# The nine taps of a 3x3 convolution, dealt out over two steps or four of a scan pipeline

## The chip, the core and the metric

The kernel runs on one core of one Trainium2 chip. The metric is the device time of one execution in microseconds (us). The chip's engines are named as in the profile: PE is TensorE's matmul and PEld its weight load, DVE is VectorE, ACT is ScalarE, POOL is GpSimd, SP is SyncE, which issues DMAs. "L468" is line 468 of the kernel before.

## What is computed

The program runs four layers, each of the form `x = x + layer(group_norm(x))`, on x of shape (8, 128, 64, 64) in float32. The change is in layer 0. Layer 0 splits the 128 channels in two halves. The first 64 go through a selective state-space scan along the 4096 pixels of an image; the last 64, `x_hw`, go through a plain 3x3 convolution. Cut to what matters:

```python
x_id, x_hw = (x[:, :GC], x[:, GC:])                  # GC = 64
t = x_id.transpose(0, 2, 3, 1) @ expand_w @ concat_w + concat_b
xs, z = split(_ln(t) @ in_w + in_b)                  # 128 channels each
xc = silu(causal_conv1d(xs))                         # 3 taps along the pixels
dt, Bm, Cm = projections(xc)                         # Bm, Cm: N = 16 states
dA  = exp(dt[..., None] * A)
dBx = dt[..., None] * Bm[:, :, None, :] * xc[..., None]
h_t = dA_t * h_{t-1} + dBx_t;  y_t = sum_n h_t[:, n] * C_t[n]
y = (y + xc * D_ssm) * silu(z)
x_id_out = (t + y @ out_w + out_b).transpose(0, 3, 1, 2)
hw = conv3x3(x_hw, conv_w) + conv_b                  # 'SAME' padding
return relu(concatenate([x_id_out, hw], axis=1))
```

Layer 1 then runs four sweeps of a 1x9 convolution over rows and columns, one row after another; layers 2 and 3 are convolutions and a deformable convolution with gathered samples.

## The kernel before

Layer 0 is worked off in 32 **chunks** of 1024 pixels (16 image rows): four chunks per image, eight images. A chunk has two halves of 512 pixels (T = 512), one PSUM bank each in float32. The scan needs 128 channels times 16 states = 2048 lanes, that is 16 groups of 128 partitions per half, and a **step** of the pipeline handles two groups. So a half takes 8 steps and a chunk 16, and the whole scan 512 steps, one after another in a single loop (L629). Chunk c owns steps 16c to 16c+15; below, "step 14" is the fifteenth of its chunk's own steps, at `t0 + 14` with `t0 = 16 * c`.

In step i, the loop issues in this order:

- `step_scan(i)` (L578): DVE multiplies the products u of the two groups with B, in PSUM (L583), and runs two scans (L594) into a tile `hb` (four buffers).
- `layer1.add(i)`: in the second half of the layer, DVE's part of a layer-1 row.
- `step_u(i + 1)` and `step_dt(i + 2)` (both through `spread`, L559): PE spreads 8 channels over 128 lanes, for u and for dt, by two products each. I call the four together the **spread products**. u has two double banks at first; from step `shared` = 280 on it has one, and the other is lent to layer 1. dt has one double bank.
- `step_carry(i - 1)` (L600, ACT): the last column of `hb`, for the next half.
- `step_decay(i + 2)` (L576): ACT takes the exponential of dt.
- `step_weigh(i - 1)` (L605): POOL multiplies `hb` with C.
- the **events** of step i (L643): everything else that has to be done for some chunk, put down beforehand in a table by `at(step, function)`.
- in odd steps, `round_sum(i - 3)` (L613): PE adds up the states of steps i-3 and i-2, four products; I call it the **group sum**. It waits for POOL's weighing, and it frees two `hb` buffers, for which the scans of steps i+1 and i+2 wait.
- `layer1.products(i)` (L724): once layer 1 has begun (step 294 on, images 0 to 3), nine products of one of its rows.

Each engine works its own queue in this order. The events of a chunk begin 33 steps before its scan (load, normalization, the products of the input side) and end 24 steps after its first scan step. So several chunks' events fall into each step. In terms of the chunk whose scan runs, PE's events by step are: ps_x in steps 0 and 1 (three products each, L386), ps_bc and ps_z in steps 2 and 3, ps_o in step 4, ps_v in 5 and 6, ps_t in 7, ps_var in 8, ps_bc again in 10 and 11, and the 3x3 convolution, ps_c, in steps 14 and 15. All these products share one PSUM bank (pool `pg`, L155, one buffer): the next may begin when an engine has read the one before. Where the chunk before was the last of its image (chunks 4, 8, 12, ...), the events of step 12 contain `out_norm` (L507), put down with the chunk before and so ahead of the chunk's own: DVE makes the mean and variance of the finished image, with two tiny products (ps_gn L272, ps_gv L280) between DVE's instructions.

The convolution (`conv_taps`, L458) takes the taps one by one, the middle one first: a tap is two products (one for each half of the chunk) of the 64 input channels in the upper 64 partitions of `xn` with a 64x64 weight, added up in ps_c. After the last tap ACT reads the two halves of ps_c into `res` (L476). Its planning is:

```python
at(t0 + 14, also(conv_taps, taps[0:5]))
at(t0 + 15, also(conv_taps, taps[5:9]))
```

## Time and profile before

| what | us |
|---|---|
| three timed runs: lowest, median, highest | 7635.89, 7638.51, 7647.05 |
| the profiled execution | 8068.85 |
| its span, first to last instruction | 8066.5 |
| layer 0's scan, from the first L583 to the last, in the profiled execution | 95.5 to 3157.4 |
| of it before layer 1 shares TensorE | to about 1600 |
| busy in the span: PE, DVE, POOL, ACT | 6262.5, 4469.1, 4114.6, 3505.2 |

The profiled execution is longer than the timed runs, so shares and durations come from it and the comparison of kernels from the timed runs. A row of the profile's groups names the line, the engine, the operation, the tiles (result first, then operands), the shape and the count, then the busy time and the mean duration, and last the engine's idle time ahead of these instructions and what ended it. A product in float32 shows as two records. "PEclk" is the clock that TensorE was granted, as a share of full speed; at 0.5 a product takes twice as long.

| groups of layer 0 | count | mean ns |
|---|---|---|
| L583 DVE, product with B | 512 | 1221 |
| L594 DVE, scan | 896 and 128 | 1267 and 1208 |
| L605 POOL, weighing with C | 512 | 2379 |
| L576 ACT, exponential | 512 | 1024 |
| L468 PE, convolution taps (two shapes) | 1152 in all | 646 and 634, overlapping |
| L476 ACT, reading ps_c | 64 | 682 |

### The profile page before, as it was taken

The page shows a single profiled execution, that of the slowest core. Times are in us where ns is not written, and L with a number is a line of the kernel's source. Part 1 is how long each engine was busy: PE and PEld are TensorE (multiplying, and loading weights), DVE is VectorE, ACT ScalarE, POOL GpSimd, SP SyncE. Part 2 cuts the span into 40 slices and gives each one's busy share as a digit, 9 for nine tenths or more (in the row PEclk, how much of TensorE's full clock was granted, in tenths as well). Part 3 has the DMA queues.
Part 4 walks back from the last instruction along what each step waited for, and adds up shares of the span by engine and source line. Part 5 has one row for each costly group of instructions (what it writes and reads, how often), then busy time and mean ns, then how long its engine had stood idle before and what let it go on. Part 6 is the DMA issues. An engine that isn't in the chain of part 4 may idle for free. (4 is left out here: it accounts for less than half of the span.)

```text
span 8066.5 us, 87137 instructions
## 1 busy us (share of the span) xinstructions
PE 6262.5 (78%) x30226; PEld 4059.5 (50%) x30226; DVE 4469.1 (55%) x5384; ACT 3505.2 (43%) x8218; POOL 4114.6 (51%) x3325
## 2 busy tenths in 40 slices
PE   6777878799999999538999999974467777676661
PEld 1222222255555556416777777753355555555551
DVE  4887887666666655111556545555445454454445
ACT  4554555433333331021444444444355555555453
POOL 3766666544444443111445444445565666666664
PEclk9887888799999999869999999987689888888785
DMA  1010110100000000131455455455566666666557
GB/s 41 26 44 26 38 36 28 35 12 24 21 19 18 17 14 9 54 118 51 150 174 160 155 163 158 152 163 172 170 201 194 207 195 201 192 199 201 177 176 259
DMA packets 333015, 897.77 MB, mean 111 GB/s; under 512 B 55464, under 2 KB 90544, under 8 KB 330528
## 3 DMA queue, kind: packets, MB, share of 16 engines
q0 software_dynamic: 184320, 604.13, 24.7%
q1 hardware_dynamic: 143648, 271.31, 10.3%
q10 hardware_dynamic: 4608, 16.78, 0.5%
q8 instruction: 239, 3.92, 0.2%
q14 instruction: 200, 1.64, 0.1%
HBM read 770.80 MB, written 121.21 MB: 111 GB/s over the span
## 5 line engine op out<-in xcount | busy, mean ns | idle before, releaser
L605 POOL TENSOR_TENSOR hb<-hb,bc 128x1024 f32<-128x1024 f32 x512 | 1216.4, 2379 | 1360.9 <-ACT carry L600 979.1
L1105 POOL DMA_INDIRECT X<-table,idx x1332 | 1272.1, 955 | 799.8 <-PE ps_s L1137 350.1
L1105 POOL DMA_INDIRECT got<-table,idx x972 | 930.0, 957 | 1083.8 <-ACT samp L1140 439.8
L594 DVE TENSOR_TENSOR_SCAN hb<-da,carry,u_ps 128x512 f32<-128x512 f32 x896 | 1098.0, 1267 | 275.8 <-PE ps_y L613 224.7
L576 ACT ACTIVATE da<-dt_ps 128x1024 f32<-128x1024 f32 x512 | 524.3, 1024 | 1316.0 <-PE dt_ps L559 1315.6
L1148 PE MATMUL ps_o<-samp,dcn_w 128*128 128x256 f32 x2304 | 676.4, 436 | 418.7 <-ACT samp L1140 224.0
L1137 PE MATMUL ps_s<-ident,X 128*128 128x128 f32 x5328 | 794.9, 308 | 241.2 <-DVE X L1123 144.7
L1140 ACT COPY samp<-ps_s 128x384 f32<-128x384 f32 x768 | 365.1, 475 | 1412.6 <-PE ps_s L1137 1033.7
L1123 DVE TENSOR_TENSOR X<-prod,X 128x768 f32<-128x768 f32 x444 | 425.2, 958 | 966.1 <-ACT X L1116 805.6
L1137 PEld LDWEIGHTS ps_s<-ident,X 128*128 128x128 f32 x5328 | 767.3, 221 | 303.1 <-DVE X L1123 161.7
L1116 ACT ACTIVATE X<-X,wgt 128x128 f32<-128x128 f32 x2664 | 826.1, 392 | 0.0
L559 PE MATMUL u_ps<-u,m_u 32*128 32x512 f32 x2048 | 639.3, 703 | 194.4 <-DVE hb L594 193.4
L1148 PEld LDWEIGHTS ps_o<-samp,dcn_w 128*128 128x128 f32 x2304 | 470.2, 214 | 554.2 <-ACT samp L1140 251.2
L583 DVE TENSOR_TENSOR u_ps<-u_ps,bc 128x1024 f32<-128x1024 f32 x512 | 625.2, 1221 | 182.1 <-PE dt_ps L559 165.3
L1116 ACT ACTIVATE got<-got,wgt 128x128 f32<-128x128 f32 x1944 | 611.2, 392 | 193.6 <-DMA got<-table,idx 189.9
L559 PE MATMUL dt_ps<-dt,m_dt 32*128 32x512 f32 x2048 | 642.5, 706 | 17.6 <-ACT da L576 17.6
L1121 DVE TENSOR_TENSOR prod<-X,prod 128x768 f32<-128x768 f32 x444 | 426.5, 961 | 117.4 <-ACT prod L1095 69.3
L1125 DVE TENSOR_TENSOR prod<-prod,got 128x384 f32<-128x384 f32 x324 | 183.6, 567 | 506.3 <-ACT got L1116 453.7
L559 PEld LDWEIGHTS u_ps<-u,m_u 32*128 32x128 f32 x2048 | 166.3, 198 | 553.2 <-DVE hb L594 365.9
L1121 DVE TENSOR_TENSOR prod<-got,prod 128x768 f32<-128x768 f32 x324 | 309.6, 955 | 145.7 <-DMA got<-table,idx 96.0
L1137 PE MATMUL ps_s<-ident,got 128*128 128x128 f32 x1944 | 296.1, 293 | 109.5 <-issue 47.6
L876 PE MATMUL ps_t<-xn,w 128*128 128x512 f32 (+4 forms) x688 | 317.3, 611 | 81.1 <-DVE t L907 56.6
(224 smaller groups left out, 10218.1 us busy)
## 6 DMA issues: line engine op xcount, KB each, us to landing
x<-x1d SPq DMA_DIRECT2D x128, 256.0 KB
table<-tok SPq DMA_DIRECT2D x128, 256.0 KB
X<-table,idx POOLq DMA_INDIRECT x1332
x<-x2d SPq DMA_DIRECT2D x48, 384.0 KB
x3h<-x3d SPq DMA_DIRECT2D x16, 1056.0 KB
x_st<-in_x SPq DMA_DIRECT2D x64, 256.0 KB
x_o<-in_x SPq DMA_DIRECT2D x64, 256.0 KB
x1d<-res SPq DMA_DIRECT2D x64, 256.0 KB
```

Source lines behind the costliest of these rows:

```text
L559: nc.tensor.matmul(ps[:, j, :], lhsT=mask[q, r].rearrange("p d n -> p (d n)"), rhs=S[c][src, h][q, :], start=True, stop=True,)
L576: nc.scalar.activation(da, steps[i]["dt"], AF.Exp)
L583: nc.vector.tensor_mul(st["bc"], st["bc"], s["bc", h][:, 0].unsqueeze(1).to_broadcast([P, 2, T]))
L594: nc.vector.tensor_tensor_scan(hb[:, j, :], st["da"][:, j, :], st["bc"][:, j, :], start, ALU.mult, ALU.add)
L605: nc.gpsimd.tensor_mul(hb, hb, S[c]["bc", h][:, 1].unsqueeze(1).to_broadcast([P, 2, T]))
L1105: nc.gpsimd.indirect_dma_start(out=got[:, k, :, :].rearrange("p q c -> p (q c)"), out_offset=None, in_=tab, in_offset=bass.IndirectOffsetO ...
L1116: nc.scalar.activation(got[:, k, q, :], got[:, k, q, :], AF.Identity, scale=wgt[:, t, k0 + k, q : q + 1])
L1121: nc.vector.tensor_mul(prod, got[:, :, 0:2, :], w.unsqueeze(3).to_broadcast([P, G3, 2, C]))
L1123: nc.vector.tensor_add(got[:, :, 0:2, :], prod, got[:, :, 2:4, :])
L1137: nc.tensor.matmul(ps[:, k, :], lhsT=got[:, k, q, :], rhs=self.ident, start=(q == 0), stop=(q == halves - 1))
L1140: nc.scalar.copy(samp[:, :, col : col + P], ps)
L1148: nc.tensor.matmul(ps, lhsT=self.dcn_w[:, k, :], rhs=samp[:, k - k0, :], start=(k == 0), stop=(k == KK - 1))
```

## The change

The nine taps are called in four parts of 3, 2, 2 and 2 taps, in steps 12, 13, 14 and 15, in place of two parts of 5 and 4 taps in steps 14 and 15. The order of the taps, the products themselves, the bank they add up in and the two ACT instructions after the last tap are the same. The bank and the tile `res` are asked for at the first part, so two steps earlier.

```diff
-                at(t0 + 14, also(conv_taps, taps[0:5]))
-                at(t0 + 15, also(conv_taps, taps[5:9]))
+                for i, ks in enumerate((taps[0:3], taps[3:5], taps[5:7], taps[7:9])):
+                    at(t0 + 12 + i, also(conv_taps, ks))
                 at(t0 + 20, y_product)
```

## The prediction

> **What bounds the kernel now.** I read the page's slices first, then engine shares by stretch, TensorE's waits, and TensorE's order of time around the convolution.

> ```profile
> PE   6777878799999999538999999974467777676661
> ...
> PEclk9887888799999999869999999987689888888785
> ```

> One digit is a fortieth of the span, 202 us. Layer 0 is the first 16 digits, in two regimes: to about 1535 us PE is 60 to 80% busy at a reduced clock, then 90% or more.

> ```profile
> core 0: us, PE busy (x) PEld busy (x) DVE busy (x) ACT busy (x) POOL busy (x), PEclk, DMA share, GB/s
> 640.00:1360.00 720.00, 575.23 (x2456) 151.62 (x2454) 589.63 (x525) 386.05 (x587) 485.09 (x254) 0.85 0.10 33
> 1658.00:3156.00 1498.00, 1464.29 (x7192) 878.49 (x7189) 923.76 (x944) 507.60 (x788) 682.79 (x357) 0.99 0.05 18
> ```

> In the first regime DVE is busy 82% and PE 80%: neither is full, so they take turns being late. In the second, where layer 1 shares TensorE (its first step is scan step 280 + 14 = 294), PE is busy 98%.

> ```profile
> PE u_ps L559 <- DVE hb L594: 170.9, 99, 4.9
> ...
> PE u_ps L559 <- DVE hb L594: 0.8, 2, 0.4
> ```

> These are TensorE's waits for the scan, first of 175 to 1535 us, then of 1658 to 3156 us (total us, times, longest). PE has holes in the first regime only. Where they lie is seen in chunk 11, steps 13 to 16:

> ```profile
> 1021.10 0.70 PE L559 MATMUL u_ps<-u,m_u 32*128 32x512 f32 x2 [1.65 <-DVE hb L594]
> ...
> 1026.14 1.05 PE L613 MATMUL ps_y<-hb,m_y 128*32 128x512 f32 x4 [2.93 <-POOL hb L605]
> ...
> 1028.20 4.47 PE L468 MATMUL ps_c<-xn,conv 64*64 64x512 f32 x20
> ...
> 1033.67 3.60 PE L468 MATMUL ps_c<-xn,conv 64*64 64x504 f32 x16
> 1037.20 1.06 PE L613 MATMUL ps_y<-hb,m_y 128*32 128x512 f32 x8
> 1038.20 0.70 PE L559 MATMUL u_ps<-u,m_u 32*128 32x512 f32 x2
> ```

> Columns: start, duration. PE idles 1.65 and 2.93 us in steps 12 and 13, then has 8.1 us of taps in steps 14 and 15. Behind them wait the spread products, and the group sum at 1037.20, which holds up the first scan of the next chunk (3.47 us of DVE idle there). Last, the granted clock:

> ```profile
> 625.00:669.00 44.00, 42.92 (x109) 11.18 (x110) 18.11 (x16) 8.19 (x16) 18.76 (x10) 0.50 0.00 1
> 1093.00:1101.00 8.00, 0.57 (x5) 0.50 (x2) 7.05 (x7) 1.22 (x2) 8.00 (x5) 0.70 0.32 102
> 1102.00:1106.00 4.00, 3.91 (x20) 0.67 (x20) 3.87 (x4) 1.60 (x4) 0.11 (x1) 0.50 0.01 4
> ```

> Third from the end is the clock. In chunk 6 PE is full for 43 of 44 us and stays at half speed. In chunk 12 the normalization of a finished image (out_norm) leaves PE idle for 8 us, and half speed follows.

> [...]43 busy us at 0.50 were taps (64 of 128 rows, 15.7 us), ps_x (64 rows, 11.0 us) and spread products between them; full speed came when ps_bc (128 rows) followed. I infer that half-height products don't release it. [...]spread products start at 1032.60, right where taps end.

> **The change part by part.** The same 36 matmul records per chunk are issued (18 products, two records each), as 12+8+8+8 in steps 12 to 15, instead of 20+16 in steps 14 and 15. One record takes 4.47/20 = 0.224 us at full clock, 8.72/20 = 0.436 at half. So 2.7 and 1.8 us of taps enter steps 12 and 13, and 2.7 and 1.8 leave steps 14 and 15. ACT's two readings of ps_c stay in step 15, no DMA is added, and the shared product bank, held two steps longer, has no other user in those steps except out_norm. Two more group switches cost at most 0.05 us each by the equal rates of the two groups, 32 x 2 x 0.05 = 3 us; I take 0, as they fall into holes or vanish beside 8 us.

> Second regime, 14 chunks: PE is full before and after, so 0. Bounds: -2 us (three out_norm holes of 0.8 us) and +3.

> First regime, an ordinary chunk, reworked from chunk 11 with 1.06 us for the spread products or a group sum. Step 12: spread to 1019.4, taps to 1022.1. Step 13: spread 1023.1, taps 1024.9, sum; its second half waits for POOL to 1026.14 as before, end 1027.1. Step 14: spread 1028.2, taps 1030.0. Step 15: spread 1031.1, taps 1032.9, sum 1033.9. The next spread starts at 1033.9, not 1038.2: 4.3 us. DVE permits it: its scans are 3.71 us apart, so step 16 can be multiplied from 1032.1. POOL's weighting of step 15 moves from 1039.0 to 1037.0, ends 1039.3, and is needed at 1041.6. Chunk 7, the same way, gives 4.0 to 5.1. I take 4.2 for 11 chunks (0 to 3, 5, 7, 9 to 11, 13, 15): 46 us. POOL is the nearest cover; if its weighting came 2.3 us later, each further us would be lost.

> Chunks 6 and 14 run taps and ps_x at half clock, because the clock fell in the hole of step 13. With taps in that hole it should not fall: the second spread after the chunk's end, at 666.16 now, comes at about 642.7: 23 us each, 46. A new phase may catch one of the 13 others instead: 20 back. Net 26 (bounds 0 and 46). Chunk 17 is at half clock too (0.50 from 1513 to 1594 us, up to layer 1's start), but the clock falls before step 12's spread, where no taps come to stand: I take 10 (bounds 0 and 30).

> Chunks 4, 8, 12, 16 have out_norm in step 12, and the order of TensorE's instructions puts the first taps right behind it: at half clock. Today the next spread, sum and spread (1101.6 to 1107, all 128 rows) release it before the taps. Afterwards, from 1101.9: taps 5.2, spread 2.0, taps 3.5, sum 1.9, spread 2.0, taps 3.5, spread 2.0, taps 3.5, sum 1.9: the next chunk's first spread at 1127.4 instead of 1117.1, and with ps_x still at half the second one after it is 18.4 us late. Should sum plus spread (3.9 us of full rows) release it earlier, the loss is 5 or 11 us; at full clock throughout it would be a gain of 1.9. With chances 0.3, 0.2 and 0.5 for 5, 11 and 18.4: 13 us each, 52 in all (bounds -8 and +74).

> Sum: 46 + 26 + 10 - 52 = 30 us gained. The profiled execution took 8068.9 us (span 8066.5, 2.4 around it), so 8039; its time is 5.6% over the median of 7638.5, and I can't see in which stage. I move the 30 us over unscaled: 7608.5.

> **The rivals.** (a) Slower: half clock becomes the rule. Taps spread over four steps thin out the full-height work that releases the clock; a chunk that enters step 12 at half speed keeps it to ps_bc. For: three of 18 chunks are caught today, steps 9 to 11 have drops. Against: of the 13 chunks outside out_norm and 17, only chunk 6 and 14 start step 12's spread at half, and recover in 0.3 us. Each catch costs 20 and the lost 4.2: two beyond the sum turn the sign; four give 30 - 97 = -67, 7705. (b) No trap behind out_norm: 46 + 46 + 10 + 8 = 110, 7528; [...]against it, chunk 6. (c) Gain eaten by the next wait: POOL works without a pause from 1023.8 to 1037.0; if its weighting sets the pace, 46 becomes about 20 and the sum 4: 7635.

> **How the numbers follow.** Forecast 0.45, (a) 0.30, (b) 0.13, (c) 0.12. The measurement tells about 0.2%, 15 us, from no change. Forecast alone: 7580 to 7640; 0.36 of it faster, 0.09 same. (b) all faster; (c) 0.02, 0.08, 0.02; (a) 0.01 same, 0.29 slower. Faster 0.51, same 0.18, slower 0.31. The range reaches halfway into (b) and to just short of (a)'s four catches: 7545 to 7695.

> **What would show it.** Right: PE's waits for the scan in steps 12 and 13 shrink, L594's wait for L613 falls from 128.9 us in the first regime, ordinary chunks are 4 us shorter; PEclk 0.50 through the taps of chunks 4, 8, 12 and 16; the stretch with layer 1 stays near 1498 us. Wrong: the first regime's length unchanged with POOL's weighting as the last release (c), or half clock through ordinary taps (a).

## The result and the profile after

The changed kernel takes 7587.9 us (median of six runs, 7574.5 to 7594.7), the kernel before on the same chip 7641.8 (six runs, 7634.7 to 7647.7): a ratio of 0.9929 with a 95% interval of 0.9916 to 0.9941, so 45 to 64 us faster. The forecast was 7608.5, a gain of 30.

The two profiled executions are 493 us apart (8068.9 and 7575.7), and most of that is not the change. Split at the last scan step, layer 0 takes 64 us less and what follows it 430 us less; in the profiles of all the runs below, what follows layer 0 takes 4480 to 4493 us in some sets of runs and 4900 to 4935 in others (the timed kernel before moved with them: 7635 to 7650 us in the first, 8039 to 8087 in the second). The record's chip numbers do not sort the two levels (chips 0 and 6 stand on both sides), so their cause stays open. Layer 0 repeats: the changed kernel's 2998.6 us came again as 3000.9, and two other kernels that were profiled twice repeat within 1 and 5 us. The kernel before was profiled once. So below I read layer 0 from the profiles, and the whole from the timed ratios.

The slices of the changed kernel, to be held against those shown of before:

```profile
PE   6888878799999999944999999998557878787760
...
PEclk9988889699999999976999999999678999999985
```

The first seven digits of the clock are 9988889 where they were 9887888. By stretch, the first regime's part without layer 1, and the second regime whole (columns as before: the third number from the end is the clock):

```profile
94.00:1462.00 1368.00, 1107.40 (x4866) 289.68 (x4862) 1178.30 (x1058) 762.98 (x1162) 967.67 (x506) 0.88 0.11 34
```

```profile
1584.00:3093.00 1509.00, 1475.36 (x7202) 878.47 (x7200) 923.70 (x944) 507.61 (x788) 683.44 (x357) 0.99 0.06 18
```

The first is chunks 0 to 17: 1368 us, against 1441 of before with the same work, at a clock of 0.88 against 0.85. The second is the stretch that took 1498 us before; it is 11 us longer. Now chunk 11 from step 12 to the next chunk, to be read beside the prediction's fence:

```profile
970.64 0.70 PE L559 MATMUL u_ps<-u,m_u 32*128 32x512 f32 x2 [1.10 <-DVE hb L594]
...
971.71 2.78 PE L468 MATMUL ps_c<-xn,conv 64*64 64x512 f32 x12
...
975.49 1.91 PE L468 MATMUL ps_c<-xn,conv 64*64 64x504 f32 x8
977.33 1.05 PE L613 MATMUL ps_y<-hb,m_y 128*32 128x512 f32 x4
978.53 1.05 PE L613 MATMUL ps_y<-hb,m_y 128*32 128x512 f32 x4 [0.15 <-POOL hb L605]
...
980.59 1.90 PE L468 MATMUL ps_c<-xn,conv 64*64 64x504 f32 x8
982.42 0.70 PE L559 MATMUL u_ps<-u,m_u 32*128 32x512 f32 x2
...
983.49 1.92 PE L468 MATMUL ps_c<-xn,conv 64*64 64x512 f32 x8
985.33 1.06 PE L613 MATMUL ps_y<-hb,m_y 128*32 128x512 f32 x8
986.33 0.70 PE L559 MATMUL u_ps<-u,m_u 32*128 32x512 f32 x2
```

The holes of steps 12 and 13 are gone: the wait ahead of the group sum's second half is 0.15 us where it was 2.93. From the spread products of step 12 to those of step 16 it takes 15.7 us (970.64 to 986.33), before 19.9 (1018.31 to 1038.20). DVE now sets the pace, with one multiplication every 3.71 us through all these steps (977.91, 981.62, 985.33). The scans' waits for the group sum (total us, times) tell the same, first before, then after, over the first regime:

```profile
  PE ps_y L613: 128.9, 63
```

```profile
  PE ps_y L613: 70.4, 54
```

And the step that the prediction feared, chunk 12 with out_norm ahead of its taps:

```profile
1049.47 0.58 PE L280 MATMUL ps_gv<-n_dm,gmat 128*128 128x1 f32 x2 [4.04 <-DVE n_dm L276]
1050.31 5.36 PE L468 MATMUL ps_c<-xn,conv 64*64 64x512 f32 x12 [0.25 <-DVE n_dm L281]
...
1057.61 3.62 PE L468 MATMUL ps_c<-xn,conv 64*64 64x441 f32 x8
1061.17 1.93 PE L613 MATMUL ps_y<-hb,m_y 128*32 128x512 f32 x8
1063.03 1.22 PE L559 MATMUL u_ps<-u,m_u 32*128 32x512 f32 x2
...
1065.05 2.09 PE L468 MATMUL ps_c<-xn,conv 64*64 64x504 f32 x8
```

Two parts of taps do run at half clock (5.36 us for 12 records, 3.62 for 8), but behind the group sum and spread products between 1061 and 1065 the clock comes back (it is 0.50 from 1045.0 to 1065.5 us), and the third part takes 2.09 us for 8.

### The profile page after: what moved, and what is told of

It is laid out like the page before. It is cut to its first block, busy times and chain, and to the rows that moved or that the text cites. A ratio compares the mean times of both kernels' runs of the same rounds, so it can differ in the third digit from the quotient of the medians.

```text
span 7573.4 us, 87138 instructions
## 1 busy us (share of the span) xinstructions
PE 6108.4 (81%) x30226; PEld 3938.9 (52%) x30226; DVE 4461.1 (59%) x5384; ACT 3513.2 (46%) x8218; POOL 4116.9 (54%) x3325
## 5 line engine op out<-in xcount | busy, mean ns | idle before, releaser
L605 POOL TENSOR_TENSOR hb<-hb,bc 128x1024 f32<-128x1024 f32 x512 | 1216.4, 2383 | 1271.9 <-ACT carry L600 893.3
L594 DVE TENSOR_TENSOR_SCAN hb<-da,carry,u_ps 128x512 f32<-128x512 f32 x896 | 1097.8, 1266 | 245.5 <-PE ps_y L613 178.4
L1137 PE MATMUL ps_s<-ident,X 128*128 128x128 f32 x5328 | 730.5, 291 | 240.5 <-DVE X L1123 189.7
L1137 PEld LDWEIGHTS ps_s<-ident,X 128*128 128x128 f32 x5328 | 697.7, 204 | 296.4 <-DVE X L1123 218.4
L1148 PE MATMUL ps_o<-samp,dcn_w 128*128 128x256 f32 x2304 | 622.2, 409 | 205.6 <-ACT samp L1140 205.6
L559 PE MATMUL u_ps<-u,m_u 32*128 32x512 f32 x2048 | 624.3, 688 | 154.1 <-DVE hb L594 153.7
L559 PE MATMUL dt_ps<-dt,m_dt 32*128 32x512 f32 x2048 | 625.3, 689 | 17.9 <-ACT da L576 17.9
L1148 PEld LDWEIGHTS ps_o<-samp,dcn_w 128*128 128x128 f32 x2304 | 440.0, 200 | 330.2 <-ACT samp L1140 250.6
L559 PEld LDWEIGHTS u_ps<-u,m_u 32*128 32x128 f32 x2048 | 164.3, 196 | 511.7 <-DVE hb L594 315.5
L732 DVE SCALAR_TENSOR_TENSOR X<-u_ps,X 128x256 f32<-128x256 f32 x252 | 106.9, 424 | 501.1 <-PE u_ps L724 500.7
```

The costliest lines, as they stand in the source:

```text
L559: nc.tensor.matmul(ps[:, j, :], lhsT=mask[q, r].rearrange("p d n -> p (d n)"), rhs=S[c][src, h][q, :], start=True, stop=True,)
L594: nc.vector.tensor_tensor_scan(hb[:, j, :], st["da"][:, j, :], st["bc"][:, j, :], start, ALU.mult, ALU.add)
L605: nc.gpsimd.tensor_mul(hb, hb, S[c]["bc", h][:, 1].unsqueeze(1).to_broadcast([P, 2, T]))
L1137: nc.tensor.matmul(ps[:, k, :], lhsT=got[:, k, q, :], rhs=self.ident, start=(q == 0), stop=(q == halves - 1))
L1148: nc.tensor.matmul(ps, lhsT=self.dcn_w[:, k, :], rhs=samp[:, k - k0, :], start=(k == 0), stop=(k == KK - 1))
```

## Time by chunk

A chunk's time is the distance from its first spread product to the next chunk's, taken from the order of time. The differences to before, in us:

| chunks | each | sum |
|---|---|---|
| ordinary: 0, 1, 2, 3, 5, 10, 11, 13 | -3.8 to -6.6, mean -5.1 | -41 |
| 6 with 7, 14 with 15 (the long half-clock stretches end in the next chunk) | -29.2 a pair | -58 |
| 9 | +3.5 | +3 |
| out_norm: 4, 8, 12, 16 | +5.6 to +5.7 | +22 |
| 17 | -0.5 | 0 |
| first regime | | -73.7 |
| second regime | +3.9, +0.5, +2.2 in chunks 20, 24, 28; 0.3 in most others; chunk 31 +2.8 | +9.6 |

Chunk 31's 2.8 us is no loss: its first taps moved ahead of the last spread product, with which I end the count. Chunk 18 takes 1.7 us less, as chunk 17's half-clock stretch runs into it. Chunk 9 is new: its taps now run at half clock (0.50 from 830 to 843 us).

## The experiments

My theory H: the taps fill holes that DVE and POOL leave in steps 12 and 13, which relieves steps 14 and 15; beside that, the clock decides over 5 to 20 us in some chunks, and it is held down by products over 64 of the 128 rows. The rivals: the clock alone gives the gain (C); only the lighter steps count (E); only the taps' place counts and not their even spreading. Layer 0 of all runs, in us from the first spread product of step 0 to that of step 511, and the whole as a ratio to the kernel before on the same chip:

| run | chunks 0 to 17 | 18 to 31 | ratio, 95% interval |
|---|---|---|---|
| before | 1442.0 | 1620.7 | 1 |
| changed | 1368.3 | 1630.3 | 0.9929 (0.9916 to 0.9941) |
| changed again | 1369.8 | 1631.1 | 0.9914 (0.9884 to 0.9945) |
| out_norm's chunks as before | 1363.7 | 1621.3 | 0.9898 (0.9867 to 0.9928) |
| only out_norm's chunks changed | 1442.8 | 1625.2 | 1.0013 (0.9994 to 1.0031) |
| before, holes filled with throwaway taps | 1431.7 | 1621.2 | 1.0001 (0.9983 to 1.0020) |
| five and four taps in steps 12 and 13 | 1412.9 | 1617.9 | 0.9966 (0.9952 to 0.9979) |
| changed, out_norm two steps earlier | 1322.4 | 1643.3 | 0.9860 (0.9820 to 0.9900) |
| changed, taps over 128 rows | 1348.2 | 1625.2 | 0.9876 (0.9836 to 0.9916) |
| before, taps over 128 rows | 1411.1 | 1615.9 | 0.9953 (0.9935 to 0.9972) |
| five and four early, over 128 rows | 1381.2 | 1621.1 | one execution, no interval |
| all three edits | 1316.9 | 1612.8 | 0.9868 (0.9805 to 0.9931) |

Below, a chunk is **caught** where its taps or the products behind them run at half clock. A **window** is 3.41 us: in each profile, the clock changes between 100 and 1520 us only at times a whole number of 3.41 us apart.

**The changed kernel again.** 

> The changed kernel again, on this chip[...]. Theory H: layer 0's scan (step 0 to the last step) takes 2999 us again as in the first profile, and the whole is 45 to 64 us faster than before. Rival (the chip's state decides): another layer 0 time, by more than 5 us.

Layer 0 took 3000.9 us against 2998.6: the time repeats within 2.3 us, so layer 0 times may be compared across runs.

**Out_norm's chunks left as they were.**

```diff
+                if c and g == 0:
+                    at(t0 + 14, also(conv_taps, taps[0:5]))
+                    at(t0 + 15, also(conv_taps, taps[5:9]))
+                else:
                     for i, ks in enumerate((taps[0:3], taps[3:5], taps[5:7], taps[7:9])):
                         at(t0 + 12 + i, also(conv_taps, ks))
```

> Four parts in all chunks except 4, 8, ..., 28, the ones that have out_norm in step 12; these keep two parts in steps 14 and 15. Theory H (the taps fill holes in steps 12 and 13 of the first regime; taps behind out_norm run at half clock and lose): the changed kernel loses 5.6 us in each of chunks 4, 8, 12, 16 and some 11 us in chunks 20, 24, 28, so this one is about 34 us faster than it: 54 + 34 = 88 us under the kernel before, about 7554. Rival C (the gain comes from the clock alone, and out_norm's chunks are longer for another reason, such as a drift of the whole pipeline): the same as the changed kernel, about 7588.

The ratio gives 82 us (58 to 108), near H's 88. In layer 0 it is 14 us under the changed kernel instead of 34. Chunks 4, 8, 12 and 16 lose nothing now (-1.1 to -1.4 instead of +5.6), and the second regime is back at 1621; but chunks 5 and 13 are caught at half clock instead (+3.1 each where they had gained 4.5), beside 9. So the price of out_norm's chunks is as told, and part of what was saved was lost elsewhere.

**Only out_norm's chunks changed.** The condition above, turned round.

> The reverse: four parts only in chunks 4, 8, ..., 28, two parts elsewhere. Theory H: only the losses remain, 22 us in the first regime and 11 in the second: about 33 us slower than before, 7675. If the prediction's full price (13 to 18 us a chunk) holds where the clock's window lies differently, up to 7720. Rival C: no difference, 7642.

The whole was 0.1% slower, with no change within the interval: less than H said. The chunks themselves lost what H said and somewhat more (+7.1, +5.6, +9.1 and +7.1, then 10 us in chunks 20, 24 and 28, half of it given back in the chunks after them), but the pipeline's shift took 30 us off chunks 6, 7, 14 and 15: the long half-clock stretch of chunk 6 is gone, and that of chunk 14 lasts 24 us instead of 44. C, which expected no loss in these chunks, falls. What I had not reckoned with is that a shift of the pipeline alone can deal the long half-clock stretches anew, as it did here.

**The holes filled, the taps left in place.** Added in chunks 1 to 3, 5 to 7, 9 to 11, 13 to 15 and 17; the products go to a throwaway tile.

```diff
+                if g and c < 18:
+                    at(t0 + 12, also(fill, taps[0:3]))
+                    at(t0 + 13, also(fill, taps[3:5]))
                 at(t0 + 14, also(conv_taps, taps[0:5]))
                 at(t0 + 15, also(conv_taps, taps[5:9]))
```

> Adds work: the taps stay in steps 14 and 15, and in chunks 1 to 3, 5 to 7, 9 to 11, 13 to 15 and 17 three taps' worth of products in step 12 and two in step 13 are computed into a throwaway tile and never read. This fills the holes without relieving steps 14 and 15. Theory H: ordinary chunks gain nothing, 0 to 1 us lost each; but the clock no longer falls in the hole ahead of the taps, so the long half-clock stretches of chunks 6 and 14 go (2 x 24): about 48 us faster, 7594. Rival C (clock alone gives all of it): as much as the changed kernel without its out_norm loss, 7550 to 7560. Rival E (the gain comes only from the lighter steps 14 and 15, the clock has no part): no gain, 7642 or slower by up to 13.

No change, where H expected 48 us. The part on chunks 6 and 14 came true: 34 us less in chunks 6, 7, 14 and 15. But chunks 5, 9, 13 and 17 took 5.6 to 7.0 us more each, 24 in all; the clock of chunk 5's taps was 0.53:

```profile
545.00:559.00 14.00, 14.00 (x46) 3.01 (x44) 8.65 (x8) 4.76 (x9) 12.33 (x8) 0.53 0.23 77
```

TensorE is full for 14 of 14 us there, and stays at half speed; the filler's products are over 64 rows like the taps. Chunks 1 to 3, 10 and 11, whose taps the clock leaves alone, moved by -1.8 to +1.5: filling the hole gives nothing unless work leaves steps 14 and 15. So C as the whole explanation falls a second time, and E is nearer the truth for ordinary chunks than "fuller holes keep the clock up".

**Five and four taps, in steps 12 and 13.**

```diff
-                at(t0 + 14, also(conv_taps, taps[0:5]))
-                at(t0 + 15, also(conv_taps, taps[5:9]))
+                at(t0 + 12, also(conv_taps, taps[0:5]))
+                at(t0 + 13, also(conv_taps, taps[5:9]))
```

This is for the chunks without out_norm; those with it keep steps 14 and 15.

> Two parts of five and four taps, but in steps 12 and 13 instead of 14 and 15; chunks with out_norm in step 12 keep steps 14 and 15. Theory H, worked through chunk 11's times: the group sum of step 13 now stands behind 8 us of taps and holds up the scan of step 14, so an ordinary chunk gains about 2 us instead of 5; the half-clock stretches of chunks 6 and 14 go (48): 68 us faster, 7574. Should only the place of the taps count and not their even spreading: as the four-part kernel with the same exception, 7554. Should only even spreading count: no gain, 7642 or slower.

A gain of 27 us (17 to 39) where H said 68 and "place only" 88. Chunks 1, 2, 8, 9 and 17 were caught at half clock (+3 to +9.5). The rest could not be judged with the clock in it, so I came back to it with the next edit.

**Taps over all 128 rows**, in the changed kernel and in the one before. The lower 64 rows of the weights are zero, so the sums stay the same and a tap's product is over 128 rows instead of 64:

```diff
+            nc.gpsimd.memset(conv[LO], 0.0)
...
-                                lhsT=conv[HI, k, :],
-                                rhs=s["xn"][HI, 1 + 8 * h + o0 + dy : 1 + 8 * h + o1 + dy, c0 + dx : c1 + dx],
+                                lhsT=conv[:, k, :],
+                                rhs=s["xn"][:, 1 + 8 * h + o0 + dy : 1 + 8 * h + o1 + dy, c0 + dx : c1 + dx],
```

> The changed kernel with the taps as products over all 128 rows: the lower 64 rows of the weights are zero, so the sums are the same. Theory H with the inferred cause (products over 64 rows don't release the half clock): after out_norm the clock comes back within two windows of 3.4 us, chunks 4, 8, 12, 16 lose 0 to 1 us instead of 5.6, chunk 9 is not caught, chunk 17 less: layer 0 some 45 us shorter than in the changed kernel. Rival (the height has no part; taps of any shape hold the clock): layer 0 the same. Rival (128 rows cost more time): ps_o's products over 128 and 64 rows take the same 1.08 us for four, so 0; were it 0.05 us a record, 58 us longer.

> The kernel before with taps over all 128 rows, in steps 14 and 15. Theory H with that cause: the long half-clock stretches of chunks 6 and 14 (44 us each) shrink to one or two windows, worth 2 x 20, and part of chunk 17's: 40 to 60 us faster than before, ordinary chunks as before. Rival (height has no part): as before, within 5 us in layer 0.

The numbers are as H had them, somewhat smaller: 25 us off the changed kernel's layer 0 (expected 45) and 36 off the one before (expected 40 to 60). But half of the 36 is luck, as is shown below. The record of a tap costs the same: 20 take 4.47 us at full clock over 64 rows (chunk 11 of the kernel before, at 1028.20) and over 128 (at 635.84 in the kernel before with full-height taps). Chunk 12 of the changed kernel with full-height taps (line numbers are one higher, since the edit adds a line):

```profile
1041.74 5.25 PE L469 MATMUL ps_c<-xn,conv 128*64 128x512 f32 x12 [0.25 <-DVE n_dm L282]
1046.92 0.70 PE L560 MATMUL u_ps<-u,m_u 32*128 32x512 f32 x2
...
1047.99 1.91 PE L469 MATMUL ps_c<-xn,conv 128*64 128x441 f32 x8
```

The first part of taps is still at half clock (5.25 us for 12 records), and full clock follows it: the next products run at full speed (0.70 us for the two of u, 1.91 for 8 taps' records), 14 us after the hole's start (1033 to 1047) instead of 24 (1041 to 1065), and chunks 4, 8, 12 and 16 cost +1.0 to +1.1 instead of +5.6 to +5.7 against before. In the kernel before, chunk 14 shows the same. Its clock falls at the same place, in the hole of step 13 (at 1256.7 us in the kernel before); here is the first part of its taps, first as it was, then with full-height taps:

```profile
1261.44 8.72 PE L468 MATMUL ps_c<-xn,conv 64*64 64x512 f32 x20
```

```profile
1250.94 5.48 PE L469 MATMUL ps_c<-xn,conv 128*64 128x512 f32 x20
```

At full height the clock is back 2 us into the taps (at half clock 20 records take 8.72 us, at full 4.47), and chunks 14 and 15 take 17.7 us less. Chunk 6, whose stretch stood at 0.50 for 44 us, is at 0.96 now, but that is not the taps' doing: the pipeline had shifted (chunk 6 begins 6 us later), the clock fell in the hole of step 12 already, at 628.4, and was back at 631.8, ahead of the first tap at 635.84. The run in which only out_norm's chunks were changed has the same stretch at 0.96 with taps over 64 rows; here are both, full-height taps first:

```profile
625.00:669.00 44.00, 37.21 (x172) 10.14 (x172) 35.45 (x31) 20.42 (x33) 30.77 (x19) 0.96 0.00 1
```

```profile
625.00:669.00 44.00, 37.71 (x178) 10.51 (x178) 35.43 (x32) 18.75 (x33) 34.56 (x20) 0.96 0.00 1
```

So the 18 us that chunks 6 and 7 take less are luck of the shift.

What the height does is clearest when all fourteen profiles are read together. Between 100 and 1520 us I counted the windows at half clock that one kind of product filled to over 97%. Taps or filler of 64 rows and 64 columns filled 44 of them, ps_x (64 rows, 128 columns) 27, and the clock stayed at half after all 71. Taps of 128 rows and 64 columns filled 9, and the clock was full after all 9. As ps_x and the full-height taps have the same number of rows times columns (64 x 128 and 128 x 64), it is the height of the products that counted in these windows, and neither how busy TensorE was nor rows times columns.

With most of the long half-clock stretches out of both kernels, the change itself is worth 1411.1 - 1348.2 = 63 us in the first regime and -9 in the second.

**Five and four taps early, at full height.** The edit of the run above and this one together.

> Five and four taps in steps 12 and 13 (14 and 15 in out_norm's chunks), over all 128 rows, so that the half clock has no part in it. To be held against the kernel before with full-height taps (chunks 0 to 17: 1411 us) and the changed one with them (1348). Theory H: an ordinary chunk gains 2 us, since the group sum behind eight us of taps holds up the scan of step 14: 14 x 2 = 28, 1383 us. Rival (only the place counts, not the even spreading): about 1411 - 14 x 4.5 = 1348.

The sum is H's number, 1381.2 us, but only in part for H's reason. The clock was not out of it: chunks 1 and 2 went to half clock in ps_x (64 rows), which follows the taps, and took 5 us more than before each; here is chunk 1's stretch:

```profile
178.00:195.00 17.00, 17.00 (x38) 4.73 (x36) 11.08 (x12) 4.44 (x7) 8.86 (x4) 0.51 0.05 16
```

In six chunks whose taps run at full clock in all three kernels, but for 2 us in one (3, 6, 7, 10, 11, 14), five and four taps early gain 4.0 us each over the kernel before with full-height taps, the four even parts 5.5. So the place in the holes gives about three quarters of an ordinary chunk's gain and even spreading a quarter, as far as six chunks of one profile each can tell; H had put the first at 2 us. In chunk 11, the stretch from step 12's spread product to step 16's takes 17.6 us with five and four early (984.57 to 1002.13), 15.7 with four parts, 19.9 before: the group sum behind two parts of taps does hold up the next scan, as H says, but the chunk makes up part of it afterwards.

**Out_norm two steps earlier**, so that ps_bc follows it and not the taps.

```diff
-                    at(t0 + 28, out_norm)
+                    at(t0 + 26, out_norm)
```

> The changed kernel with out_norm two steps earlier (step 10 of the next chunk, ahead of ps_bc, not of the taps). Theory H: the same 8 us hole, but full-height ps_bc and a group sum follow it, so the taps of chunks 4, 8, ... run at full clock and those chunks gain as ordinary ones: some 10 us each in the first regime (42) and 9 to 11 us in all in the second: layer 0 about 50 us shorter than in the changed kernel. Rival: what costs is the hole itself, wherever it stands: layer 0 within 10 us of the changed kernel's.

In the first regime it took 46 us off the changed kernel, as H had it (42): chunks 4, 8, 12 and 16 now gain 4.1 to 4.3, chunk 9 gains 3.3. After out_norm come ps_bc and the group sum, both over 128 rows, with spread products (32 rows) between them, and the clock is full before the taps (1.06 us for the group sum's 8 records, 2.78 for 12 of the taps):

```profile
1013.03 2.07 PE L441 MATMUL ps_bc<-act,w_bc 128*128 128x512 f32 x2 [0.25 <-DVE n_dm L281]
1015.03 1.22 PE L559 MATMUL u_ps<-u,m_u 32*128 32x512 f32 x2
...
1018.73 1.06 PE L613 MATMUL ps_y<-hb,m_y 128*32 128x512 f32 x8
...
1020.79 2.78 PE L468 MATMUL ps_c<-xn,conv 64*64 64x512 f32 x12
```

The hole is not "the same 8 us", as was expected: TensorE waits 2.47 and 2.36 us in it (3.51 and 4.04 in the changed kernel), so some 3 of the 10 us that these chunks gain come from a shorter hole, and the run does not test the other products behind it alone.

In the second regime it did the reverse of what was expected: 13 us longer than the changed kernel, with +5.0, +6.5 and +6.4 in chunks 20, 24 and 28. TensorE waits 3.56 us ahead of ps_gv in each of them, where it waited 0.70, for two DVE instructions of one element per partition (L275, L276). In the changed kernel's chunk 20 they take 0.16 and 0.22 us. Here they take 2.05 and 1.19, and each ends with the POOL instruction beside it:

```profile
1734.42 2.34 POOL L605 TENSOR_TENSOR hb<-hb,bc 128x1024 f32<-128x1024 f32 x1 [7.87 <-issue]
1734.73 2.05 DVE L275 TENSOR_TENSOR n_dm<-mv,norm 128x1 f32<-128x1 f32 x1
1736.73 1.26 POOL L433 TENSOR_TENSOR xz<-xz 128x512 f32<-128x512 f32 x1
1736.82 1.19 DVE L276 SCALAR_TENSOR_TENSOR n_dm<-n_dm,mv 128x1 f32<-128x1 f32 x1
```

The holes of the first regime hold the same pair (1.45 and 2.26 us in the changed kernel's chunk 12). In the fourteen profiles, up to 3300 us, DVE instructions that write n_dm take more than 0.3 us 317 times, and each time they end within 0.06 us of the end of a POOL instruction. That POOL holds DVE up is read from these times alone; no run takes POOL's work away.

**All three.** Four parts and the earlier out_norm in chunks before step 280 only, full-height taps throughout.

```diff
+                early = 16 * c < shared
+                if early:
                     for i, ks in enumerate((taps[0:3], taps[3:5], taps[5:7], taps[7:9])):
                         at(t0 + 12 + i, also(conv_taps, ks))
+                else:
+                    at(t0 + 14, also(conv_taps, taps[0:5]))
+                    at(t0 + 15, also(conv_taps, taps[5:9]))
...
-                    at(t0 + 28, out_norm)
+                    at(t0 + (26 if early else 28), out_norm)
```

> Four parts and out_norm two steps earlier in the chunks before scan step 280, two parts and the old out_norm after it, and taps over all 128 rows throughout. Theory H: the first regime takes the best of both runs, 1318 to 1325 us for chunks 0 to 17 (1322 with the earlier out_norm, less some 4 in chunk 17), the second 1616 to 1621 as before; layer 0 some 125 us shorter than before, 7510 against 7635: a ratio of 0.984. Rival (the two cures overlap and each disturbs the clock elsewhere): not below the run with the earlier out_norm alone, ratio 0.986 to 0.988.

> The kernel with all three edits again, beside the one with the earlier out_norm alone, on one chip, since the first time its interval was 1.3% wide. From the profiles of layer 0 (133 us shorter than before; the other one 97): a ratio to before of 0.9826[...], and 36 us less than the other.

> The changed kernel with out_norm two steps earlier, again, as the partner of the run with all three edits: 97 us less than before, a ratio of 0.9873.

Layer 0 took 2929.7 us (2934.2 the second time), 133 and 129 less than before, somewhat better than the 125 expected; the first regime's clock is 0.91, where it was 0.85 before. The first ratio, 0.9868, was too wide to tell H from its rival. Side by side on one chip, this kernel took 7517.0 us (7507.4 to 7530.6) and its partner with the earlier out_norm alone 7542.8 (7535.7 to 7554.0); ratios to before 0.9822 (0.9795 to 0.9849) and 0.9852 (0.9826 to 0.9878). The two intervals overlap at their edges, but no run of the one was as slow as the fastest of the other. Layer 0's 31 to 36 us between them are near the 26 of the medians. By its ratio this kernel is 1.5 to 2.1% faster than the kernel before, and the changed kernel is 0.6 to 0.8%.

## Why the prediction was right, and where its sizes were off

Direction, place and the main mechanism were right, and the time lies in the range; the gain was 54 us (45 to 64), not 30. That says little, as the range ran from 7545 to 7695. In layer 0 the profiles show 64 us, more than twice the sum of 30; nearly the whole of the difference is out_norm's term, and the other errors cancel. Term by term:

- **Ordinary chunks, 4.2 us each.** Measured 5.1. Of chunk 11's rework (next spread 15.6 us after step 12's) the trace shows 15.7, with the group sum waiting 0.15 us for POOL. POOL's weighting did not become the pace (rival c); DVE's 3.71 us did. How place and even spreading share it, about three to one, was not in the prediction; the five-and-four kernels show it.
- **Chunks 6 and 14, 46 less 20 for a new catch.** Taking 5.1 for each of the four chunks concerned, the pairs' 58 us leave 19 for each long stretch, so 24 each with the ordinary part; the forecast was 23. The new catch was chunk 9: 8.6 us from -5.1 to +3.5, not 20 and more, as its half clock lasted 14 us and not 44. The long stretches are missing in all eight profiles with four parts in these chunks; but a shift alone can end one too (chunk 6, above), so how much of this is due to the filled hole is not shown.
- **Chunk 17, 10 us.** Measured 0.5, or 2.2 with chunk 18, into which its stretch runs. It stays at half clock (0.50 for 55 us now, 82 before).
- **Out_norm's chunks, 13 us each.** This is the term that was mis-sized most: 5.6 each, 22 instead of 52. The mechanism was right (taps at 0.5 clock behind the hole); of the three cases, the mildest (5 us, release by sum plus spread at the end of step 13) came in all four, where I had given it 0.3. The step behind it was also misread: of the "3.9 us of full rows" only the group sum's 1.9 are over 128 rows, as a spread product is over 32 (32*128 in its record). So full clock came back after less full-height work than I had thought necessary. Likewise, the prediction's account of the 43 us in chunk 6 leaves out three group sums of 1.9 us, which did not end the half clock there. My estimate from the windows of 3.41 us is that the price depends on how one falls on the group sum and its neighbours: chunks 4, 8, 12 and 16 lost 5.6 to 5.7 alike, but 5.6 to 9.1 when only these chunks were changed.
- **Second regime, 0.** Measured +9.6, of which 2.8 is the count's end. Two steps failed. "PE is full before and after, so 0" overlooked out_norm: with a hole of only 0.9 us and the taps right behind it, the clock fell there too, to 0.50 from 1795.9 to 1802.7 us in chunk 20 and from 2748.2 to 2751.6 in chunk 28, but not in 24. Chunk 20's first part took 3.99 us for 2.7, and the layer-1 products behind it 6.14 for 4.0:

```profile
1794.48 3.99 PE L468 MATMUL ps_c<-xn,conv 64*64 64x512 f32 x12 [0.25 <-DVE n_dm L281]
1798.41 6.14 PE L724 MATMUL u_ps<-X,w_down 128*128 128x256 f32 x18
```

  And the switches between groups, put at 0, are not free: from start to the next group's start, chunk 11's four parts take 2.71 + 1.84 + 1.83 + 1.84 = 8.22 us, the two parts took 4.40 + 3.53 = 7.93. The 0.3 us appears in most chunks of the full second regime.

That TensorE was busy was not enough to bring full clock back: of the 3.41 us windows at half clock full of 64-row products, 71 of 71 were followed by half clock (and in the filled chunk 5 TensorE was full for 14 us on end at 0.53), of those full of the same taps over 128 rows, 9 of 9 by full clock. What a window has to hold is not settled by that: windows that TensorE filled to over 95% with more than one kind of product went both ways (44 to full clock and 15 to half in the kernel before, 45 and 22 in the changed one), and other data were not tried.

The chance of 0.30 for "half clock becomes the rule" had a true core: a catch moved with the shifts of these runs (chunks 5 and 13 in one run, 1, 2, 8, 9 and 17 in another). In the changed kernel only chunk 9 was added.

## What to carry to other kernels

Where two engines take turns being late, look for the steps in which one idles and move a burst there in small parts; keep each part shorter than the slower engine's step, and ask which sum or release stands behind it on its queue. Before pricing the move, look at the granted clock: here taps over 64 rows put right behind an idle stretch ran at half speed (5.36 us for 12 records, 2.78 elsewhere), and full clock came back behind products over all 128 rows (1.93 us of the group sum, or a first part of full-height taps). Padding the rows with zero weights cost no time here (4.47 us for 20 records at either height). Moving the idle stretch ahead of other work was the better cure where TensorE had holes (46 us against 20 in the first regime), and a loss of 13 us where it was full.
